# Seven quarter products in place of eight for the feed-forward weight product of the last three groups

## The chip, the core and the metric

The kernel runs on one core of a Trainium2 chip. The metric is the device time of one execution, in microseconds (us). All arithmetic is in 32-bit floats. The five engines have queues of their own: TensorE (PE in the profile) multiplies matrices into PSUM, VectorE (DVE), ScalarE (ACT) and GpSimd (POOL) work element by element, and SyncE (SP) issues DMA transfers.

## The reference, cut to what matters

Two layers work on 2 x 1024 tokens of width 256. Each layer has a cross-attention and a feed-forward step. The step that matters here is the first layer's feed-forward, in which the tokens are cut into 8 groups of 256, each with weights of its own, and nothing nonlinear stands between the two products:

```python
xg = x.reshape(8, 256, 256)
h1 = einsum('gmh,goh->gmo', xg, W1) + b1[:, None, :]     # W1: 8 x 1024 x 256
h2 = einsum('gmo,gho->gmh', h1, W2) + b2[:, None, :]     # W2: 8 x 256 x 1024
x = x + h2                                               # xg is layernorm(x)
```

So the two weights of a group can be multiplied once, into a matrix M of 256 x 256 (summed over the 1024 inner features), and the group's tokens then need one product with M. Before it stands the first layer's attention, behind it the second layer's attention over 64 context rows and a slot feed-forward with soft dispatch and combination.

## The kernel before, in words

**Tiling.** Tokens lie in four quads `xq[q]` of 128 partitions x 4 tiles x 256 features; a quad holds two feed-forward groups. A group's weights come as one tile `wg` of 128 partitions x 8 chunks (`oc`) x 513 elements: 256 elements of the first weight (`w1g`, the bias b1 folded into its first column), 256 of the second (`w2g`), and one column that is subtracted from the first weight by `prepare` (line 869, eight ScalarE instructions for each group from the second on). Three buffers take the eight groups in turn, so the load of a group waits until the product three groups earlier is done.

**The weight product.** `product(g)` makes M in PSUM: for each of 8 chunks and each of 2 halves of the rows, one TensorE matmul with a 128x128 block of `w1g` as the stationary operand and 128x256 of `w2g` streaming (line 882), 16 in all. A 32-bit matmul shows as two rows in the trace, so a product counts 32. Then one copy moves M to the SBUF tile `mt` (line 890), GpSimd adds b2 to one row (line 891), and `prepare` works on the next group.

**What stands around it.** The program is written as one sequence of calls; a scheduler moves the instructions of each engine within it by their dependences, except where an order is kept by hand. The part that matters runs as follows:

```python
        product(4); load_layer1(); norm_ff(1); attend(3)
        product(5); feed_forward(1)
        product(6); norm_ff(2); feed_forward(2)
        slot_norms(); norm_queries(0); product(7)
        norm_ff(3); norm_queries(1); norm_queries(2)
```

`norm_ff(q)` makes a layernorm of a quad on VectorE (`hn_f`, with the reciprocal root `rstd` on GpSimd, lines 124 and 125) and turns it by TensorE (`pt_f`). `feed_forward(q)` multiplies it with the two M of the quad (line 910) and adds the result to the tokens on VectorE (line 917). `norm_queries(q)` is the next layernorm (`hn_a`): VectorE normalizes (line 818) and turns 32x32 squares (`tr_a`, line 137); SyncE moves those out to DRAM (`d_a`, line 170) and back (`hTa`, line 172).

**The attention loop behind it.** For each quad it runs over two halves c. `queries` makes `pq` (line 1240) and the scores `psg` (line 1308), ScalarE takes a tanh, TensorE makes `poT` (line 1340), VectorE writes that to `oT` (line 1347), and `output` multiplies `oT` of both halves with the output weight into `pf` (line 1254), which VectorE adds to the tokens (line 1262). In the first quad's second half stands `norm_queries(3)`, kept in program order, ahead of the `oT` of that half on VectorE.

**The same scheme elsewhere.** The last feed-forward already makes its products by seven quarter products. `sum_rights` (lines 607 to 615) makes sums of quarters there with four VectorE instructions of 128x512, and the products have 128 columns (line 586).

Of the kernel before, what the change touches and what calls it, by code (L numbers as in the profile page):

```python
# [9 lines left out]
FP = mybir.dt.float32  # L10
AF = mybir.ActivationFunctionType
ALU = mybir.AluOpType
# [3 lines left out]
P = 128  # L16
B = 2
S = 1024
D = 256
DC = D // P  # L20
# [14 lines left out]
OC = FF // P  # L35
# [17 lines left out]
def tile_kernel(  # L53
# [19 lines left out]
    nc = tc.nc  # L73
# [9 lines left out]
    def bank(name, side=0):  # L83
        return ps[side].tile([P, 512], FP, tag="bank", name=name)
# [511 lines left out]
    def tt(dst, x, y, op):  # L596
        nc.vector.tensor_tensor(dst, x, y, op)  # L597
# [201 lines left out]
    with (  # L799
# [34 lines left out]
        ffc = wide.enter_context(tc.tile_pool(name="ffc", bufs=1))  # L834
        weights = {}

        def load_group(g, parts=(OC,)):


            wg = wff.tile([P, OC, 2 * D + 1], FP, tag="wg", name=f"wg_{g}")  # L840
            i = 0
            for n in parts:
                nc.sync.dma_start(out=wg[:, i : i + n], in_=wff_in[g, :, i : i + n])
                i += n
            weights[g] = wg[:, :, 0:D], wg[:, :, D : 2 * D], wg[:, :, 2 * D :]
# [10 lines left out]
        def prepare(g):  # L856
            if g not in weights:
                load_group(g)
            w1g, _, first = weights[g]
            less = ffc.tile([P, OC], FP, name=f"less_{g}")  # L860
            for part, scalar in enumerate((g > 0, g > 0)):
                ocs = range(part * OC // 2, (part + 1) * OC // 2)
                some = slice(ocs.start, ocs.stop)
                if scalar:
                    nc.scalar.activation(less[:, some], first[:, some, 0], AF.Copy, scale=-1.0)
                for oc in ocs:
                    w = w1g[:, oc, 1:]
                    if scalar:
                        last_prepared[g] = nc.scalar.activation(  # L869
                        w, w, AF.Identity, bias=less[:, oc : oc + 1]  # L870
                    )
                    else:
                        nc.vector.tensor_scalar(w, w, first[:, oc, :], None, ALU.subtract)  # L873

        def product(g):
            if g == 0:
                prepare(0)
            w1g, w2g, _ = weights[g]
            pm = bank(f"pmt_{g}", 1)
            for oc in range(OC):  # L880
                for hc in range(DC):
                    nc.tensor.matmul(  # L882
                        pm[:, ts(hc, D)],
                        lhsT=w1g[:, oc, ts(hc, P)],
                        rhs=w2g[:, oc, :],
                        start=(oc == 0 and hc == 0),
                        stop=(oc == OC - 1 and hc == DC - 1),
                    )
            mt = ffc.tile([P, DC, D], FP, name=f"mt_{g}")
            nc.any.tensor_copy(mt, pm.rearrange("p (c n) -> p c n", c=DC))  # L890
            nc.gpsimd.tensor_tensor(mt[0:1, 0, :], mt[0:1, 0, :], b2r[:, g, :], ALU.add)
            mts.append(mt)
            if g + 1 < NG:
                prepare(g + 1)


        hTfs = {}

        def norm_ff(q, side=0):
            out = nc.any.tensor_copy if q < QB else nc.scalar.copy  # L900
            hTfs[q] = layernorm(xq[q], f"f0_{q}", side, out)

        def feed_forward(q, side=0):
            for i in range(QN // GN):
                g = q * (QN // GN) + i
                xg = xq[q][:, ts(i, 2), :]
                po = bank(f"po_{g}", side)
                for t in range(2):
                    for dc in range(DC):
                        nc.tensor.matmul(  # L910
                            po[:, ts(t, D)],
                            lhsT=hTfs[q][:, dc, ds(i * GN + t * P, P)],
                            rhs=mts[g][:, dc, :],
                            start=(dc == 0),
                            stop=(dc == DC - 1),
                        )
                nc.vector.tensor_tensor(
                    xg, xg, po.rearrange("p (t d) -> p t d", t=2), ALU.add
                )
# [7 lines left out]
        with tc.tile_pool(name="p0", bufs=1) as p0, tc.tile_pool(name="a0", bufs=2) as a0:  # L927
# [25 lines left out]
            load_quad(3)  # L953

            product(0)


# [22 lines left out]
            for c in range(C0):  # L980
                for dc in range(DC):
                    nc.tensor.matmul(
                        pk[:, ts(c, P)],
                        lhsT=wk0s[:, dc, ts(c, P)],
                        rhs=hcT[:, dc].rearrange("p b j -> p (b j)"),
                        start=(dc == 0),
                        stop=(dc == DC - 1),
# [5 lines left out]
            for c in range(C0):  # L993
                for dc in range(DC):
                    nc.tensor.matmul(
                        pv[:, ts(c, P)],
                        lhsT=wv0s[:, dc, ts(c, P)],
                        rhs=hcT[:, dc].rearrange("p b j -> p (b j)"),
                        start=(dc == 0),
                        stop=(dc == DC - 1),  # L1000
# [9 lines left out]
            for dc in range(DC):  # L1010
                pws = [bank(f"pwk_{dc}_{e}") for e in range(2)]
                for c in range(C0):
                    for e in range(2):
# [3 lines left out]
                            lhsT=wq0s[r, c, ts(dc, P)],  # L1017
                            rhs=kT[r, c, :],
                            start=True,
                            stop=True,  # L1020
# [8 lines left out]
            for g in range(NBW // 2):  # L1029
                pw = bank(f"pvw_{g}")  # L1030
                for i in range(2):
                    for c in range(C0):
                        nc.tensor.matmul(
                            pw[ds(32 * c, 32), ts(i, D)],
                            lhsT=vblk[:, c, 2 * g + i].rearrange("p e j -> p (e j)"),
                            rhs=wo0s[:, c, :],
                            start=True,
                            stop=True,
# [52 lines left out]
            def turn_weights(q):  # L1091
                atf = ats[q].rearrange("p g j -> p (g j)")
                pat = bank(f"pat_{q}")
                for t in range(QT):
                    nc.tensor.transpose(pat[:, ts(t, P)], atf[:, ts(t, P)], ident)
                atT = a0.tile([P, QN], FP, tag="atT", name=f"atT_{q}")
                nc.scalar.copy(atT, pat)
                atTs[q] = atT

            def attend(q):  # L1100
                if q not in atTs:
                    turn_weights(q)
                atT = atTs[q]
                for i in range(2):
                    po = bank(f"po0_{q}_{i}")
                    for k in range(2):
                        t = 2 * i + k
                        nc.tensor.matmul(  # L1108
                            po[:, ts(k, D)],
                            lhsT=atT[:, ts(t, P)],  # L1110
                            rhs=vw[:, (q * QT + t) // 2, :],
                            start=True,
                            stop=True,
                        )
                    xi = xq[q][:, ts(i, 2), :]
                    nc.vector.tensor_tensor(
                        xi, xi, po.rearrange("p (t d) -> p t d", t=2), ALU.add
                    )

            weigh(0)  # L1120
            product(1)
            turn_weights(0)
            weigh(1)
            attend(0)
            product(2)
            turn_weights(1)
            weigh(2)
# [7 lines left out]
            load_layer1()  # L1135
            norm_ff(1)
            attend(3)
        product(5)
        feed_forward(1)
        product(6)  # L1140
        norm_ff(2)
        feed_forward(2)

        with (
            tc.tile_pool(name="a1c", bufs=1, side="right") as a1c,
# [35 lines left out]
            for c in range(C1):  # L1181
                for dc in range(DC):
                    nc.tensor.matmul(
                        pk[:, ts(c, P)],
                        lhsT=wk1s[:, dc, ts(c, P)],
                        rhs=ctxd[:, dc],
                        start=(dc == 0),
                        stop=(dc == DC - 1),
# [13 lines left out]
            for dc in range(DC):  # L1202
                nc.tensor.matmul(
                    pv[:, 0:D],
                    lhsT=ctxd[:, dc].rearrange("p b s -> p (b s)"),
                    rhs=wv1s[:, dc, :],
                    start=(dc == 0),
                    stop=(dc == DC - 1),
# [5 lines left out]
            for b in range(B):  # L1214
                for e in range(2):
                    to = vblk1[e * NK : (e + 1) * NK, b, :, e, :]
# [63 lines left out]
            for c in range(C1):  # L1280
                nc.tensor.matmul(
                    pvs[:, ts(c, B)],
                    lhsT=vals[:, ts(c, NPR)].rearrange("p r e d -> p (r e d)"),
                    rhs=in_batch,
                    start=True,
                    stop=True,
# [7 lines left out]
            for q in range(NQ):  # L1294
                b = q * QN // S
                oTs[q] = a1.tile([P, C1, QN], FP, tag="oT", name=f"oT_{q}")
                for c in range(C1):
# [8 lines left out]
                    for j in range(NPR):  # L1306
# [3 lines left out]
                            lhsT=kblk[r, c, b].rearrange("p e s -> p (e s)"),  # L1310
                            rhs=qTs[q][r, c, :],
                            start=True,
                            stop=True,
# [25 lines left out]
                    for j in range(NPR):  # L1339
                        nc.tensor.matmul(  # L1340
                            po[ds(32 * j, 32), :],
                            lhsT=vblk1[:, b, NPR * c + j].rearrange("p e d -> p (e d)"),
                            rhs=sg[:, j, :],
                            start=True,
                            stop=True,
# [153 lines left out]
```

## Time and profile before

| | |
|---|---|
| median of 3 runs | 423.4 us (423.31 to 423.4) |
| the profiled execution's own time | 423.25 us |
| its span, first to last instruction | 421.5 us |
| TensorE busy | 415.9 us, 99% of the span |
| VectorE busy | 315.6 us, 75% |
| ScalarE busy | 131.1 us, 31% |
| GpSimd busy | 74.1 us, 18% |
| granted TensorE clock | 1.000 |
| `pmt` matmuls of all 8 products (line 882) | 256 rows, 58.3 us |
| products 5, 6 and 7 on TensorE | start at 69.80, 82.03 and 95.37 us, 6.91 us each |

The span is the time that the profile sees; 1.75 us of the execution lie around it. Busy times are sums over the whole span; the durations of TensorE rows are modelled and overlap, so the distance from start to start says more than a row's own duration. In a row of the timeline stand the start, the time from first start to last end of its instructions, the engine, the source line, the operation with the tile that it writes and the tiles that it reads, their shapes, the count, and in brackets the idle time ahead of it with what ended it.

### The profile page before, as it was taken

The page shows a single profiled execution, that of the slowest core. Times are in us where ns is not written, and L with a number is a line of the kernel's source. Part 1 is how long each engine was busy: PE and PEld are TensorE (multiplying, and loading weights), DVE is VectorE, ACT ScalarE, POOL GpSimd, SP SyncE. Part 2 cuts the span into 40 slices and gives each one's busy share as a digit, 9 for nine tenths or more (in the row PEclk, how much of TensorE's full clock was granted, in tenths as well). Part 3 has the DMA queues.
Part 4 walks back from the last instruction along what each step waited for, and adds up shares of the span by engine and source line. Part 5 has one row for each costly group of instructions (what it writes and reads, how often), then busy time and mean ns, then how long its engine had stood idle before and what let it go on. Part 6 is the DMA issues. An engine that isn't in the chain of part 4 may idle for free.

```text
span 421.5 us, 6298 instructions
## 1 busy us (share of the span) xinstructions
PE 415.9 (99%) x2270; PEld 310.3 (74%) x2270; DVE 315.6 (75%) x711; ACT 131.1 (31%) x266; POOL 74.1 (18%) x86
## 2 busy tenths in 40 slices
PE   8999999999999999999999999999999999999996
PEld 7889988888444454444488644899998864499996
DVE  2677777745578669978769889977985589776956
ACT  1145938513544522344641654300000004420000
POOL 2113233211101220104948900000000000000000
PEclk9999999999999999999999999999999999999999
DMA  6999983413633332120052764450022576520003
GB/s 256 416 415 425 402 340 134 168 47 112 149 102 105 46 47 31 29 43 2 0 213 101 129 97 74 65 89 2 0 84 49 121 120 98 89 44 2 2 2 100
DMA packets 99425, 50.03 MB, mean 119 GB/s; under 512 B 87873, under 2 KB 94401, under 8 KB 97857
## 3 DMA queue, kind: packets, MB, share of 16 engines
q1 hardware_dynamic: 99394, 49.63, 42.2%
q8 instruction: 18, 0.29, 0.3%
q14 instruction: 13, 0.11, 0.1%
HBM read 32.74 MB, written 6.30 MB: 93 GB/s over the span
## 4 chain that ended last, share of the span: by engine, by line
PE 86%; DVE 7%; SPq 2%; DMA 2%; issue 1%; POOL 1%; ACT 0%; DVEq 0%
PE psl L409 13%; PE pmt L882 13%; PE pc L586 12%; PE pp L586 12%; PE pmh L511 10%; PE pl L256 7%; PE pq L1240 3%; PE po L910 3%; SPq L158 2%; PE psc L1058 2%; PE pf L1254 2%; PE po L1108 2%; PE psg L1308 2%; PE poT L1340 1%; DMA wg<-in_wff_dram 1%
## 5 line engine op out<-in xcount | busy, mean ns | idle before, releaser
L882 PE MATMUL pmt<-wg 128*128 128x256 f32 x256 | 58.3, 384 | 0.3 <-DVE wg L873 0.3
L409 PE MATMUL psl<-xh,lg 128*128 128x258 f32 x256 | 56.8, 381 | 0.0
L256 PE MATMUL pl<-seT,xhT 128*128 128x512 f32 x128 | 56.1, 594 | 0.2 <-DVE rmax L275 0.2
L882 PEld LDWEIGHTS pmt<-wg 128*128 128x128 f32 x256 | 48.8, 193 | 7.5 <-DVE wg L873 0.7
L409 PEld LDWEIGHTS psl<-xh,lg 128*128 128x128 f32 x256 | 48.2, 190 | 7.4 <-issue 0.5
L256 PEld LDWEIGHTS pl<-seT,xhT 128*128 128x128 f32 x128 | 24.1, 190 | 29.2 <-issue 25.7
L395 POOL TENSOR_TENSOR lg<-lg,mb 128x1024 f32<-128x1024 f32 x13 | 33.2, 2594 | 26.9 <-ACT mb L203 25.3
L279 ACT ACTIVATE ec<-lg,nm 128x1024 f32<-128x1024 f32 x16 | 18.4, 1149 | 39.7 <-DVE nm L264 37.7
L586 PEld LDWEIGHTS pp<-ms,mh 128*128 128x128 f32 x256 | 29.4, 192 | 1.6 <-issue 1.0
L586 PE MATMUL pp<-ms,mh 128*128 128x128 f32 x256 | 30.2, 276 | 0.3
L521 ACT ACTIVATE mh<-mh 128x512 f32<-128x512 f32 x32 | 19.2, 627 | 21.1 <-DVE mh L557 19.6
L511 PE MATMUL pmh<-slT,ms 128*128 128x512 f32 x48 | 24.2, 592 | 0.0
L869 ACT ACTIVATE wg<-wg,less 128x255 f32<-128x255 f32 x56 | 23.4, 495 | 0.1
L1317 ACT ACTIVATE sg<-psg 128x512 f32<-128x512 f32 x32 | 16.5, 603 | 18.2 <-PE psg L1308 18.2
L586 PE MATMUL pp<-m_sums,mh 128*128 128x128 f32 x192 | 22.1, 275 | 0.0
L586 PE MATMUL pc<-pr,ec 128*128 128x128 f32 x192 | 22.1, 275 | 0.0
L586 PEld LDWEIGHTS pc<-pr,ec 128*128 128x128 f32 x192 | 21.8, 192 | 0.0
L586 PEld LDWEIGHTS pp<-m_sums,mh 128*128 128x128 f32 x192 | 21.8, 192 | 0.0
L398 ACT ACTIVATE lg<-lg 128x1024 f32<-128x1024 f32 x16 | 16.1, 1045 | 18.3 <-POOL lg L395 18.3
L545 ACT COPY mh<-pmh 128x512 f32<-128x512 f32 x8 | 4.6, 569 | 50.2 <-PE pmh L511 50.2
L308 DVE STREAM_TRANSPOSE tr<-ec 128x512 f32<-128x512 f32 x32 | 19.7, 674 | 0.0
L597 DVE TENSOR_TENSOR mh<-mh,mh 128x1024 f32<-128x1024 f32 x16 | 18.5, 1218 | 0.5 <-PE pp L586 0.5
(193 smaller groups left out, 669.8 us busy)
## 6 DMA issues: line engine op xcount, KB each, us to landing
wg<-in_wff_dram SPq DMA_DIRECT2D x5, 2052.0 KB, 10.1
ec<-tr SPq DMA_DIRECT2D x128, 64.0 KB, 2.3
wg<-in_wff_dram SPq DMA_DIRECT2D x4, 1026.0 KB, 12.9
xT<-in_xT_dram SPq DMA_DIRECT2D x4, 512.0 KB, 13.9
x<-in_x_dram SPq DMA_DIRECT2D x4, 512.0 KB, 16.1
d_a<-tr_a SPq DMA_DIRECT2D x4, 512.0 KB, 2.6
hTa<-d_a SPq DMA_DIRECT2D x16, 128.0 KB, 3.1
xhT<-tr_m SPq DMA_DIRECT2D x64, 32.0 KB, 2.0
```

The source lines that it names most:

```text
L256: nc.tensor.matmul(pl, lhsT=xhTs[q][:, dc, ts(t, P)], rhs=in_order(seT[:, n], dc), start=(dc == 0), stop=(dc == DC - 1),)
L279: nc.scalar.activation(ecs[q][:, :, t, :], lg.rearrange("p (h n) -> p h n", h=2), AF.Exp, bias=nm[:, 1:2], scale=-1.0, accum_out=zcs[b][:, ...
L308: ins = nc.vector.transpose(tr[:, :, :, t, :].rearrange("p r c n -> p c r n"), half[:, t, :].rearrange("p (c r n) -> p c r n", c=EC // 2, ...
L395: engine.tensor_tensor(lgs[b][s], lgs[b][s], mbs[b], ALU.add)
L409: nc.tensor.matmul(pz[:, 0:XW], lhsT=lgs[b][s][:, ts(c, P)], rhs=xhs[b * QB + s // QT][:, s % QT, :], start=(s == 0), stop=(s == ST - 1),)
L511: nc.tensor.matmul(to, lhsT=lefts[i][:, ts(j, P)], rhs=in_order(slTs[b][0], i) if i < 2 else rights[b][i], start=True, stop=True,)
L521: nc.scalar.activation(h, h, AF.Gelu)
L586: nc.tensor.matmul(to, lhsT=left(k, m), rhs=right[:, k, :], start=(k == 0), stop=(k == QT - 1),)
L597: nc.vector.tensor_tensor(dst, x, y, op)
L869: last_prepared[g] = nc.scalar.activation(w, w, AF.Identity, bias=less[:, oc : oc + 1])
L882: nc.tensor.matmul(pm[:, ts(hc, D)], lhsT=w1g[:, oc, ts(hc, P)], rhs=w2g[:, oc, :], start=(oc == 0 and hc == 0), stop=(oc == OC - 1 and hc ...
L1317: nc.scalar.activation(sg[:, j, :], psgs[j], AF.Tanh, scale=0.5 * DH1**-0.5)
```

## The change

For groups 5, 6 and 7, M is no longer summed from 16 matmuls of 256 columns. Both weights are cut into quarters: by halves of the 8 chunks and by halves of their 256 columns. `sum_quarters(g)` makes the sums and differences of quarters on VectorE, eight instructions of 128x512, four of the second weight and four of the first. Two of the eight are written over a quarter of the weight itself, six into a new tile `qs`. `product_of_quarters(g)` makes seven products of quarters, each of four matmuls of 128 columns, 28 in all, in two PSUM banks. ScalarE copies the first product to SBUF, and seven VectorE additions of 128x128, each with one operand in PSUM, put the four quarters of `mt` together. `sum_quarters(g + 1)` is called at the end of `product(g)`, behind `prepare(g + 1)`. The `qs` of groups 5 and 7 share a buffer of the pool `ffc`; that of group 6 lies in a new pool `qp`, which is opened ahead of `product(5)` and closed behind `feed_forward(2)`.

```diff
+        FEWER = (5, 6, 7)
+        HO = OC // 2
+        quarter_sums, sums_in = {}, [ffc]
+        def quarters(w):
+            return [[w[:, ts(k, HO), ts(i, P)] for i in range(2)] for k in range(2)]
+        def sum_quarters(g):
+            w1g, w2g, _ = weights[g]
+            qs = sums_in[-1 if g == 6 else 0].tile([P, 6, HO, P], FP, tag="qs", name=f"qs_{g}")
+            s1, s2, s4, t1, t2, t4 = (qs[:, i] for i in range(6))
+            (b11, b12), (b21, b22) = quarters(w2g)
+            tt = nc.vector.tensor_tensor
+            tt(t1, b12, b11, ALU.subtract)
+            tt(t2, b22, t1, ALU.subtract)
+            tt(b12, b22, b12, ALU.subtract)
+            tt(t4, b21, t2, ALU.subtract)
+            (a11, a21), (a12, a22) = quarters(w1g)
+            tt(s1, a21, a22, ALU.add)
+            tt(s2, s1, a11, ALU.subtract)
+            tt(a21, a11, a21, ALU.subtract)
+            tt(s4, a12, s2, ALU.subtract)
+            quarter_sums[g] = [
+                (a11, b11), (a12, b21), (s2, t2), (a21, b12), (s1, t1), (s4, b22), (a22, t4)
+            ]
+        def product_of_quarters(g):
+            pms = [bank(f"pmt_{g}_{i}", 1) for i in range(2)]
+            p1, p2, p6, p7, p5, p3, p4 = (
+                pms[i // 4][:, ts(i % 4, P)] for i in range(7)
+            )
+            for to, (left, right) in zip((p1, p2, p6, p7, p5, p3, p4), quarter_sums[g]):
+                for k in range(HO):
+                    nc.tensor.matmul(to, lhsT=left[:, k, :], rhs=right[:, k, :],
+                                     start=(k == 0), stop=(k == HO - 1))
+            mt = ffc.tile([P, DC, D], FP, name=f"mt_{g}")
+            u = ffc.tile([P, 3, P], FP, tag="u", name=f"u_{g}")
+            (c11, c12), (c21, c22) = [[mt[:, c, ts(i, P)] for i in range(2)] for c in range(2)]
+            u1, u2, u3 = (u[:, i] for i in range(3))
+            tt = nc.vector.tensor_tensor
+            nc.scalar.copy(u1, p1)
+            tt(u2, p6, u1, ALU.add)
+            tt(c11, p2, u1, ALU.add)
+            tt(u3, p7, u2, ALU.add)
+            tt(c22, p5, u3, ALU.add)
+            tt(u2, p5, u2, ALU.add)
+            tt(c12, p3, u2, ALU.add)
+            tt(c21, p4, u3, ALU.add)
+            return mt
...
         def product(g):
...
+            if g in FEWER:
+                mt = product_of_quarters(g)
+            else:
                 pm = bank(f"pmt_{g}", 1)
...
             if g + 1 < NG:
                 prepare(g + 1)
+                if g + 1 in FEWER:
+                    sum_quarters(g + 1)
...
+        qp = ExitStack()
+        sums_in.append(qp.enter_context(tc.tile_pool(name="qp", bufs=1)))
         product(5)
         feed_forward(1)
         product(6)
         norm_ff(2)
         feed_forward(2)
+        qp.close()
```

More of the change, by code (lines that the diff above doesn't have):

```diff
@@ new lines, in product_of_quarters @@
+        def product_of_quarters(g):
[5 more added lines that the diff above has]
+                for k in range(HO):
+                    nc.tensor.matmul(
+                        to,
+                        lhsT=left[:, k, :],
+                        rhs=right[:, k, :],
+                        start=(k == 0),
+                        stop=(k == HO - 1),
+                    )
+            mt = ffc.tile([P, DC, D], FP, name=f"mt_{g}")
[12 more added lines that the diff above has]
+            return mt
@@ L878, in product @@
             w1g, w2g, _ = weights[g]
[L879 to L890, printed above, removed]
+            if g in FEWER:
+                mt = product_of_quarters(g)
+            else:
+                pm = bank(f"pmt_{g}", 1)
+                for oc in range(OC):
+                    for hc in range(DC):
+                        nc.tensor.matmul(
+                            pm[:, ts(hc, D)],
+                            lhsT=w1g[:, oc, ts(hc, P)],
+                            rhs=w2g[:, oc, :],
+                            start=(oc == 0 and hc == 0),
+                            stop=(oc == OC - 1 and hc == DC - 1),
+                        )
+                mt = ffc.tile([P, DC, D], FP, name=f"mt_{g}")
+                nc.any.tensor_copy(mt, pm.rearrange("p (c n) -> p c n", c=DC))
             nc.gpsimd.tensor_tensor(mt[0:1, 0, :], mt[0:1, 0, :], b2r[:, g, :], ALU.add)
```

## The prediction

> **What bounds the kernel now.** I read the page's shares first, then the chain of waits for 76 to 125 us, then VectorE's timeline for the same time, since what the change adds lies there.
>
> ```profile
> PE 415.9 (99%) x2270; PEld 310.3 (74%) x2270; DVE 315.6 (75%) x711; ACT 131.1 (31%) x266; POOL 74.1 (18%) x86
> ```
>
> TensorE has hardly a gap in the span: what it saves is time won, as long as nothing else makes it wait. The chain runs through it without a break in the changed stage (start, length, what):
>
> ```profile
> 82.03 6.91 PE pmt L882 x32
> ...
> 95.37 6.91 PE pmt L882 x32
> ...
> 113.82 3.63 PE pq L1240 x8
> 117.45 1.00 PE poT L1340 x8
> 118.45 1.07 PE psg L1308 x8
> 119.52 3.65 PE pf L1254 x16
> ...
> 290.11 25.01 PE pc L586 x224
> ```
>
> VectorE has room there, but it is in pieces that wait for TensorE (in brackets), and in short ones that wait for GpSimd's root:
>
> ```profile
> 60.10 0.69 DVE L1070 TENSOR_TENSOR e<-psc,mx 128x512 f32<-128x512 f32 x1
> ...
> 89.92 1.56 DVE L818 TENSOR_SCALAR hn_a<-x,mv_a,rstd_a 128x256 f32<-128x256 f32 x4 [6.17 <-PE pt_f L133]
> ...
> 103.53 0.16 DVE L1288 TENSOR_SCALAR vsum<-pvs 128x4 f32<-128x4 f32 x1 [3.58 <-PE pvs L1281]
> ...
> 110.07 0.69 DVE L917 TENSOR_TENSOR x<-x,po 128x512 f32<-128x512 f32 x1 [3.46 <-PE po L910]
> ...
> 115.74 1.38 DVE L818 TENSOR_SCALAR hn_a<-x,mv_a,rstd_a 128x256 f32<-128x256 f32 x4 [1.48 <-POOL rstd_a L125]
> ...
> 118.59 0.75 DVE L1347 TENSOR_SCALAR oT<-poT,vsum 128x512 f32<-128x512 f32 x1
> ```
>
> The last row is the second half of `oT`. It ends at 119.34, and the second matmul of `pf`, which needs it, starts at 119.52 + 0.43 = 119.95: VectorE is ready with 0.6 us to spare.
>
> **TensorE's side.** A product is 16 matmuls in 6.91 us, 0.432 each. A 128-column matmul with a new stationary block each time is in the row of `pc`: 224 rows are 112 matmuls in 25.01 us, 0.2233 each. 28 of them take 6.25 us. Each product is shorter by 0.66 us, three by **1.98 us**. That is 0.66 less than the eighth of each product (0.86): two half-width matmuls cost more than one wide. No order but the products' changes on TensorE. `pf` would start at 117.54, and its second matmul at 117.97, if nothing makes it wait.
>
> **VectorE's side.** Three groups add 24 sums of 128x512 and 21 additions of 128x128. The price is from start to start, since neighbours overlap:
>
> ```profile
> 247.32 0.68 DVE L561 TENSOR_TENSOR mh<-mh,pmh 128x512 f32<-128x512 f32 x1
> 247.92 0.68 DVE L563 TENSOR_TENSOR mh<-mh,pmh 128x512 f32<-128x512 f32 x1
> ...
> 266.19 0.68 DVE L610 TENSOR_TENSOR m_sums<-ms 128x512 f32<-128x512 f32 x1
> 266.91 1.42 DVE L597 TENSOR_TENSOR m_sums<-ms,m_sums 128x512 f32<-128x512 f32 x2
> 268.24 0.68 DVE L597 TENSOR_TENSOR ms<-ms 128x512 f32<-128x512 f32 x1
> 268.84 2.48 DVE L308 STREAM_TRANSPOSE tr<-ec 128x512 f32<-128x512 f32 x4
> ```
>
> An independent one starts 0.60 after the one before. One that reads its neighbour's result starts 0.72 after it; the last four lines are the same four-instruction pattern of sums elsewhere, 2.65 us or 0.66 each. In the changed order other work stands between most dependent pairs, so I take 0.60, with 0.66 as the dear end: 24 x 0.60 = **14.4 us** (15.8). There is no 128x128 `TENSOR_TENSOR` in the trace. From 512 to 256 columns the distance falls from 0.60 to 0.33 (`ggb`, 68.76 to 69.09), which goes on to 0.20 at 128; the three-operand form with 128 columns (line 750) takes 15 in 4.29 us, 0.28 each. I take 0.20, the same operation, and keep 0.28: 21 x 0.20 = **4.2 us** (5.9).
>
> Now the queue from line 1070's start at 60.10 to the second `oT`. Before, its instructions at these distances sum to 34.5 us: 20 `BN_STATS` at 0.32, 20 aggregates at 0.09, 24 of lines 818 at 0.315, 20 turned squares at 0.345, 4 `se` at 0.40, 15 of 512 columns at 0.61, and 1.0 of small ones. The rest of 58.5 us is standing: 16.0 us in six waits ahead of TensorE work or `sn`, 5.9 in four waits of 1.47 for `rstd`, 2.1 in gaps below 0.8. After, one copy of `hT_f` (0.6) goes to ScalarE: 34.5 - 0.6 + 14.4 + 4.2 = **52.5 us**. The added work does not just fill the gaps: it makes the queue late, so every wait for TensorE goes. The waits for `rstd` don't, because in the changed order little stands between each `mv` and its `hn`: five of them, 1.45 for `hn_f` of quad 2, 1.05 for `hn_f` of quad 3 (three small instructions between), 1.15 for `hn_a` 1, 1.4 for `hn_a` 2 (GpSimd first adds b2 to `mt` 7, 0.72), 1.45 for `hn_a` 3: 6.5 us. Short gaps: 1.0, fewer than before as there are fewer waits. The second `oT` starts at 60.10 + 52.5 + 6.5 + 1.0 = **120.1**, ends at 120.85, and the second `pf` matmul goes at 120.9 in place of 119.95. So **+0.95 us**: TensorE gains 1.98 by 117.97 and then waits 2.9 us. What is behind `oT` in VectorE's queue is the addition of `pf` itself, which comes as much later; the order behind it is that of before, so the 0.95 goes through to the end.
>
> [...] The rows at 247.32 and 247.92 start 0.60 apart with 0.68 each, so I go by the rows.
>
> **What else moves.** Within products, TensorE needs the sums from the third quarter product on. Counting the queue on: group 5's eighth sum ends near 69 (needed at 74), group 6's `s2` near 81.8 and the last near 82.8 (needed at 83.1), group 7's near 90.5 (needed at 95.5). Group 6 has 1.3 us of cover; a wait there costs nothing more until it passes the 2.9 us that TensorE loses anyhow. ScalarE: three copies of 128x512 (0.59) become three of 128x128; `sq` of `slot_norms` now waits for the last `po0` at 72.5, since its memory is used until then, so `wg` 6 is prepared near 79.3 in place of 75.4, 2 us before product 6. GpSimd: the clearing of `vblk` (0.52) and three small ones move behind the same `po0`; nothing needs them before 95. SyncE: `tr_a` 0 ends near 91.5 in place of 74.9, so `d_a` 0 and `hTa` 0 go out then, with `vblk`'s two moves now between; at 3.2 us and 3.1 us to landing and 0.43 an issue, `hTa` 0 lands near 101, and `pq` 0 wants it at 101.5. `hTa` 1 lands near 111.3 for 111.8. Both may cost some tenths, inside the same 2.9 us. PSUM: a product holds two of four banks, and `po` 6 waits for the last addition into `mt` 7, near 105 for 106.
>
> **The rivals.**
> - *Dear additions.* At 0.66 and 0.28 the queue is 1.4 + 1.7 us later: +2.6 to +4.1 us, 426.0 to 427.5. For it: PSUM operands, many dependent pairs. Against: rows of line 917 with PSUM (0.68) cost as much as those without. Chance 0.23; beyond +4.1 another 0.03, if quarters at a pitch of 513 elements ran like the slow one of `sl_sums` (line 498, 1.41 against 0.69 for its twin).
> - *VectorE in time (the other side).* If the second `oT` ends by 118.0, 2.9 us earlier than counted, TensorE keeps all 1.98: 421.3 us. It is faster by over 0.2% (0.85 us, about what a measurement can tell from no change) once `oT` ends by 119.1, 1.8 earlier. The place is the queue between 95 and 120, where 6.5 us are waits for GpSimd: two of them covered by sums would do. For it: only 5% of the queue's 60 us are in question. Against: the order is fixed, and between these `mv` and `hn` it has no sums. Chance of +0.0 down to -0.85 0.10, of less 0.07.
> - *No saving at all.* If a 128-column matmul were paced by its own duration (275 ns against 379), products would be 1.6 us longer. The chain's distances exclude it.
>
> **How the numbers follow.** The sum is made against the profiled execution's own 423.25 us, which is 0.15 below the median: 424.2 to 424.4, so 424.4. Cases: +0.0 to +1.9 around the count 0.57 (0.27 of it within 0.85), dear 0.23 + 0.03, in time 0.17. Faster 0.07, the same 0.10 + 0.27 = 0.37, slower 0.30 + 0.26 = 0.56. The range goes from -0.4 (some of the in-time case) to the dear end at +3.7 us: 423.0 to 427.1.
>
> **What would show it.** Right: three products of 6.25 us, starting near 69.8, 81.4 and 94.0; VectorE waiting only for `rstd` from 66 to 120; sums 0.60 and additions 0.20 apart; a wait of 2 to 4 us of `pf` for `oT`, line 1347 becoming line 1412, and none of over 1 us before it. Wrong: a product longer than 6.5 us with waits for `qs`, waits for `hTa`, or `pf` starting before 119.

## The result, and the profile after

The changed kernel took 428.74 us (median of 426.52, 429.94, 429.46 and 428.02), the kernel before 423.36 in the same session: ratio 1.0124, 95% interval 1.0078 to 1.0169. It is slower, and the median lies above the forecast range. Run again later, the same kernel gave 426.25 us in six executions (424.61 to 427.87) against 423.25, ratio 1.0069 (1.0052 to 1.0087); that median lies inside the range. Executions of the kernel before lie within 0.4 us of its median; those of the changed one spread over 5.3 us. That spread is the first sign of what the forecast lacked.

The profiled execution of after took 426.52 us with a span of 424.6, against 423.25 and 421.5. From the page, the shares and the row of the granted clock:

```profile
PE 415.6 (98%) x2342; PEld 311.8 (73%) x2342; DVE 333.2 (78%) x755; ACT 130.9 (31%) x267; POOL 74.9 (18%) x86
...
PEclk9999999999989999999999999999999999999999
```

The clock row has an 8 in its twelfth slice of forty, 117 to 127 us; the page of before has only nines. TensorE's timeline of after (start, length, what, and the idle time ahead of it):

```profile
81.57 1.95 PE L910 MATMUL pmt<-wg 128*128 128x128 f32 x16
...
94.21 1.95 PE L910 MATMUL pmt<-wg 128*128 128x128 f32 x16
...
117.79 0.70 PE L1319 MATMUL pf<-w1s,oT 128*128 128x256 f32 x2
121.60 4.97 PE L1319 MATMUL pf<-w1s,oT 128*128 128x256 f32 x14 [3.11 <-DVE oT L1412]
```

In the same view of before, all 16 rows of `pf` stand in one piece:

```profile
119.45 3.72 PE L1254 MATMUL pf<-w1s,oT 128*128 128x256 f32 x16
```

Up to `pf` TensorE is 1.7 us ahead of before (117.79 against 119.45). Then it stands for 3.11 us, waiting for the second `oT`. And then something that no step of the forecast has: the other 14 rows of `pf` take 4.97 us. At full clock 14 such rows take 3.29 (the run with three sums in experiment 2). The stretches around that place, from the view by windows (columns: stretch and its length, then busy time and instructions of TensorE, its weight loads, VectorE, ScalarE, GpSimd; the granted clock; the DMA share and rate):

```profile
120.00:121.50 1.50, 0.00 (x0) 0.00 (x0) 1.50 (x4) 0.00 (x0) 0.00 (x0) 1.00 0.01 1
121.50:123.00 1.50, 1.40 (x5) 1.17 (x6) 0.05 (x1) 0.00 (x0) 0.00 (x0) 0.72 0.84 339
123.00:125.00 2.00, 2.00 (x6) 1.65 (x5) 0.91 (x2) 0.00 (x0) 0.00 (x0) 0.50 0.12 33
125.00:127.00 2.00, 2.00 (x14) 1.10 (x13) 1.14 (x5) 0.00 (x0) 0.00 (x0) 0.86 0.71 227
```

The clock falls to 0.50 behind the wait. The stretches at its edges show a mean (0.72 over 1.5 us, 0.86 over 2.0); with 0.50 in the slow part, it was halved from 122.16 to 125.56, 3.40 us. The account of this execution against before: the second matmul of `pf` starts at 121.60 instead of one matmul after 119.45, at 119.88, so +1.7, of which 0.3 was there at 57.9 us already, ahead of the first sum; the 14 rows at a slow clock add 4.97 - 3.29 = 1.7. That is +3.4 at the end of `pf`; the span is 3.1 longer.

VectorE's queue, in its timeline of after:

```profile
77.67 0.28 DVE L923 TENSOR_TENSOR u<-pmt,u 128x128 f32<-128x128 f32 x1
77.87 0.27 DVE L924 TENSOR_TENSOR mt<-pmt,u 128x128 f32<-128x128 f32 x1
...
78.27 0.67 DVE L891 TENSOR_TENSOR wg<-wg 128x512 f32<-128x512 f32 x1
78.86 0.68 DVE L892 TENSOR_TENSOR qs<-wg,qs 128x512 f32<-128x512 f32 x1
...
81.19 1.23 DVE L895 TENSOR_TENSOR qs<-qs,wg 128x512 f32<-128x512 f32 x1
82.34 0.69 DVE L896 TENSOR_TENSOR wg<-wg 128x512 f32<-128x512 f32 x1
...
118.20 1.38 DVE L818 TENSOR_SCALAR hn_a<-x,mv_a,rstd_a 128x256 f32<-128x256 f32 x4 [1.48 <-POOL rstd_a L125]
...
120.84 0.71 DVE L1412 TENSOR_SCALAR oT<-poT,vsum 128x512 f32<-128x512 f32 x1
```

Sums start 0.60 apart and additions, each with an operand in PSUM, 0.20; a sum right behind the one whose result it reads starts 0.72 after it (61.00 and 61.72 us). The queue is full but for the waits for `rstd`, and the second `oT` starts 0.7 us behind the count of 120.1 (0.6 in the second profile, at 120.71).

**Theories.** *Clock theory*: a TensorE wait of about 3 us costs its length and also a halved clock for one or more stretches like the 3.40 us of this profile, each worth up to 1.7 us (half of it); how many differs from one execution to the next. By an estimate from the mean clocks of the four executions (0.996, 0.988, 0.992 and 0.992, over spans of 425 to 428 us) they had one, three, two and two such stretches at half the clock. *Rival*: the loss lies in the sums and additions or in the changed order, and the clock only accompanies it.

### The profile page after: what moved, and what is told of

It is laid out like the page before. It is cut to its first block, busy times and chain, and to the rows that moved or that the text cites. A ratio compares the mean times of both kernels' runs of the same rounds, so it can differ in the third digit from the quotient of the medians.

```text
span 424.6 us, 6494 instructions
## 1 busy us (share of the span) xinstructions
PE 415.6 (98%) x2342; PEld 311.8 (73%) x2342; DVE 333.2 (78%) x755; ACT 130.9 (31%) x267; POOL 74.9 (18%) x86
## 4 chain that ended last, share of the span: by engine, by line
PE 68%; DVE 19%; SPq 4%; DMA 3%; POOL 2%; issue 2%; ACT 0%; DVEq 0%; POOLq 0%
PE pc L586 12%; PE pp L586 11%; PE psl L409 10%; PE pmh L511 9%; PE pl L256 7%; PE pmt L942 6%; SPq L158 2%; PE pf L1319 2%; SPq L325 2%; PE psc L1120 2%; PE pq L1305 2%; DMA wg<-in_wff_dram 1%; DVE tr_a L137 1%; DVE lg L264 1%; DVE hn_a L818 1%
## 5 line engine op out<-in xcount | busy, mean ns | idle before, releaser
L942 PE MATMUL pmt<-wg 128*128 128x256 f32 x160 | 36.6, 385 | 0.7 <-DVE wg L873 0.7
L942 PEld LDWEIGHTS pmt<-wg 128*128 128x128 f32 x160 | 30.4, 193 | 5.6 <-DVE wg L873 1.4
L1319 PE MATMUL pf<-w1s,oT 128*128 128x256 f32 x64 | 17.4, 422 | 3.2 <-DVE oT L1412 3.1
L1319 PEld LDWEIGHTS pf<-w1s,oT 128*128 128x128 f32 x64 | 12.8, 208 | 10.1 <-DVE oT L1412 4.4
```

What stands on the lines that cost most here:

```text
L942: nc.tensor.matmul(pm[:, ts(hc, D)], lhsT=w1g[:, oc, ts(hc, P)], rhs=w2g[:, oc, :], start=(oc == 0 and hc == 0), stop=(oc == OC - 1 and hc ...
L1319: nc.tensor.matmul(pf[:, ts(k, D)], lhsT=oTs[q][:, c, ts(2 * i + k, P)], rhs=wo1s[:, c, :], start=(c == 0), stop=(c == C1 - 1),)
```

## The experiments

**1. The wait filled.** The changed kernel with work for TensorE where it stood:

```diff
                     pf = bank(f"pf_{q}_{i}", 1)
+                    if q == 0 and i == 0:
+                        for _ in range(14):
+                            nc.tensor.matmul(pf[:, 0:P], lhsT=wo1s[:, 0, 0:P],
+                                             rhs=wo1s[:, 1, 0:P], start=True, stop=True)
```

> The changed kernel, with 14 added matmuls of 128x128 float32 (14 x 0.223 = 3.1 us) on TensorE in the place of its wait at the first `pf`; they write into the `pf` bank that the real matmuls then write anew. Nothing is made earlier: the second `oT` still ends near 121.5 us. Clock theory: the clock stays 1.00 behind it, the 14 real `pf` matmuls take 3.2 us instead of 4.97, and the time is 424.5 to 425.1 us with runs within 0.5 us. Rival (the clock has nothing to do with the wait): 427 to 430 us and the same scatter as the changed kernel.

Measured: 425.26 us (425.07 to 425.60, five executions), ratio to before 1.0047 (1.0035 to 1.0059). Mean clock 1.000 in all five. TensorE's timeline of it:

```profile
117.52 3.39 PE L1319 MATMUL pf<-w1s 128*128 128x128 f32 x28
120.74 3.87 PE L1328 MATMUL pf<-w1s,oT 128*128 128x256 f32 x16
```

The second `oT` is about as late as without the filling (it starts at 120.55, there at 120.84), yet more work on TensorE makes the kernel 1 to 3.5 us faster than its two medians, and the spread is gone (the kernel before took 423.25 to 423.36 in the three sessions). All five executions kept the clock; unfilled, three of ten did (experiment 4), and these took 424.61 to 426.09, so the filling takes away the slow clock and not the wait's length. The rival said 427 to 430; it falls. The time is 0.2 above the upper end expected.

**2. Sums alone, without any product of seven.** In the kernel before, with n = 3, 5, 6 or 9:

```diff
-                    nc.vector.tensor_scalar(
-                        oTs[q][:, c, :], po, 0.5, vsum[:, c, b : b + 1], ALU.mult, ALU.add
+                    if c == 1 and q == 0:
+                        for _ in range(n):
+                            tc.keep_in_program_order(nc.vector.tensor_tensor(
+                                oTs[0][:, 1, :].rearrange("p (t d) -> p t d", t=2),
+                                xq[0][:, 0:2, :], xq[0][:, 2:4, :], ALU.add))
+                    tc.keep_in_program_order(nc.vector.tensor_scalar(
+                        oTs[q][:, c, :], po, 0.5, vsum[:, c, b : b + 1], ALU.mult, ALU.add
+                    ))
```

> The kernel before, with 3 sums of 128x512 on VectorE (0.60 us apart, 1.8 us) right ahead of the second `oT`, whose place they write and which writes over them; TensorE's work is unchanged. The second `oT` has 0.6 us of slack, so TensorE waits 1.2 us at `pf`. Both theories: 1.2 us more than before, 424.3 to 424.7 us. Clock theory further: a wait this short leaves the granted clock at 1.00 and the runs within 0.5 us; if it halved too, 426 us or more with scatter.

> The kernel before, with 6 such sums (3.6 us) ahead of the second `oT`: a wait of 3.0 us at `pf`, as long as the changed kernel's, without any product of seven. Clock theory: granted clock of 0.5 for some 3.4 us behind the wait, 1.7 us and more above the wait: 428 to 431 us, with runs over 1 us apart. Rival (the wait costs only its length): 426.3 us, runs within 0.5 us, clock 1.00.

> The kernel before with 5 sums ahead of the second `oT`. The six took 4.28 us (0.72 us apart) and made TensorE wait 3.42 us, so five make it wait 2.7 us. By the length alone (no clock): 423.25 + 2.7 = 425.9 to 426.2 us. Clock theory: somewhere between the 1.25 us that left the clock at 1.00 and the 3.1 us that did not, it starts to fall; if 2.7 us is enough, executions at 0.996 lie 1.7 us higher, at 427.6 or so, beside others at 426.

> The same with 9 sums: 9 x 0.72 = 6.4 us, a wait of 5.6 us at `pf`. By the length alone 428.9 to 429.3 us, all runs within 0.5 us. Clock theory: every execution loses at least one stretch of half the clock, so no mean clock above 0.997 and 430.5 to 434 us, with scatter in steps of some 1.7 us.

The row of `pf` behind its wait, in TensorE's timelines with 3, 5 and 9 sums (with 6 it is 4.78 us behind 3.42):

```profile
121.31 3.29 PE L1254 MATMUL pf<-w1s,oT 128*128 128x256 f32 x14 [1.25 <-DVE oT L1355]
```

```profile
122.84 4.94 PE L1254 MATMUL pf<-w1s,oT 128*128 128x256 f32 x14 [2.70 <-DVE oT L1355]
```

```profile
125.78 4.90 PE L1254 MATMUL pf<-w1s,oT 128*128 128x256 f32 x14 [5.60 <-DVE oT L1355]
```

| sums | wait, us | time, us (lowest to highest) | above before | mean clock of the executions |
|---|---|---|---|---|
| 3 | 1.25 | 424.33 (424.19 to 424.45) | 1.1 | 0.999 to 1.000, all 8 |
| 5 | 2.70 | 427.36 (425.50 to 428.66) | 4.1 | one 1.000, four 0.995 to 0.996, one 0.991 |
| 6 | 3.42 | 428.02 (426.97 to 429.04) | 4.8 | one 1.000, two 0.996, one 0.992 |
| 9 | 5.60 | 431.03 (430.24 to 431.89) | 7.8 | 0.992, all 4 |

A wait of 1.25 us costs 1.1 us and nothing else, so keeping the order of every `oT` by hand, which the edit also does, costs nothing of its own. With 2.70, 3.42 and 5.60 us the same 14 rows take 4.94, 4.78 and 4.90 us instead of 3.29, and the median is 1.3 to 2.2 us above the wait's length. With 2.70 and 3.42 us a single execution each kept the clock, and it cost its wait within 0.5 us (425.50 and 426.97). So the seven-product change is not needed for the effect; a late `oT` is enough. Six sums took 4.28 us and not the 3.6 expected of them, hence a wait of 3.42 for 3.0; their median lies at the low end of the clock theory's figure.

The mean clock alone does not give the price. In the profile with nine sums, by windows:

```profile
121.50:123.00 1.50, 0.00 (x0) 0.00 (x0) 1.43 (x3) 0.13 (x1) 0.00 (x0) 0.75 0.39 96
...
129.00:131.00 2.00, 2.00 (x12) 1.30 (x14) 1.69 (x6) 0.00 (x0) 0.00 (x0) 0.98 0.00 0
```

With 0.50 in all windows between, the clock was halved from 122.2 to 129.1, 6.8 us, twice the 3.40 of the first profile. For the first 3.5 us of it TensorE stood anyway, so the 14 rows are no slower than with five sums. The lowest time, 430.24 us, is 0.3 below what the clock theory had expected.

**3. Six sums, and the wait filled** with the 14 matmuls of experiment 1.

> The same with 6 sums, and with 14 added matmuls of 128x128 (3.1 us) on TensorE in the place of the wait, overwritten by the real ones. The second `oT` is as late as without them. Clock theory: clock 1.00, the time rises by the lateness alone: 426.2 to 426.8 us, runs within 0.5 us, and 2 us or more under the same kernel unfilled. Rival: the same time as unfilled.

Measured: 427.14 us (426.91 to 427.64), mean clock 0.999 to 1.000 in all four. The level is 0.3 above the range expected, for the longer six sums; it is what the unfilled kernel took in its one execution at full clock (426.97). The median falls by only 0.9 where 2 or more was expected, since of the four unfilled executions one lost nothing and only one had a clock as low as 0.992. The direction speaks for the clock theory, the size is smaller than I wrote.

**4. The changed kernel again.**

> The changed kernel again, unaltered, for more executions and a second profile. Clock theory: the executions differ by their mean granted clock, and each 0.004 of it (1.7 us of a span of 425 us) costs about 1.7 us above a floor of some 425 us, which is what the filled kernel takes at 1.000; the profile shows one or more stretches of about 3.4 us at half the clock behind the wait at `pf`. Rival: differences in time without a difference in clock, or a low clock that stands elsewhere than behind the wait.

All ten executions of it, by mean granted clock: 1.000: 424.61, 425.61, 426.09; 0.996: 426.41, 426.49, 426.52; 0.992: 427.87, 428.02, 429.46; 0.988: 429.94 us. The groups do not overlap; their means are 425.4, 426.5, 428.5 and 429.9, 1.0 to 2.0 us apart for each 0.004. The new profile is of the one at 0.992, by windows:

```profile
120.00:121.50 1.50, 0.01 (x1) 0.01 (x1) 1.43 (x4) 0.00 (x0) 0.00 (x0) 0.77 0.01 1
...
125.00:127.00 2.00, 2.00 (x6) 1.58 (x5) 1.11 (x5) 0.00 (x0) 0.00 (x0) 0.50 0.77 228
127.00:129.00 2.00, 2.00 (x14) 0.55 (x17) 1.14 (x3) 0.00 (x0) 0.00 (x0) 0.84 0.02 5
```

A wait of 3.01 us, about the same as in the first profile, and here the clock is halved from 120.8, while TensorE still stands, to 127.6: 6.8 us, twice 3.4. The 14 rows of `pf` take 6.30 us. So the length of the wait alone does not decide between one stretch and two. What does, no run shows. At clock 1.000 the kernel still spreads over 1.5 us, which the theory does not explain.

**5. The change for two groups.** `FEWER = (6, 7)`.

> The change for groups 6 and 7 alone (two products of seven, 16 sums and 14 additions). TensorE gains 2 x 0.66 = 1.3 us; VectorE has about 8 x 0.60 + 7 x 0.20 = 6.2 us less added to its queue, which is more than the 3.1 us by which it came late. Clock theory: no wait at `pf`, clock 1.00, 421.9 to 422.3 us. Rival (the cost sits in the sums and additions themselves, in proportion): two thirds of the changed kernel's loss, 425 to 427 us.

Measured: 422.06 us (421.74 to 422.23), ratio 0.9968 (0.9957 to 0.9980), mean clock 0.999 to 1.000. `oT` starts at 117.17, and TensorE runs through `pf` without a gap:

```profile
118.03 3.72 PE L1319 MATMUL pf<-w1s,oT 128*128 128x256 f32 x16
```

It gains 1.24 us of the 1.32 that two shorter products are worth, and is faster than both kernels. Two thirds of the change do not cost two thirds of the loss: that rival falls too.

**6. The norm moved out of the way**, in the changed kernel and in the kernel before.

```diff
                 for c in range(C1):
-                    if c == 1 and q == 0:
-                        norm_queries(3, True)
...
-                    nc.vector.tensor_scalar(
+                    ot = nc.vector.tensor_scalar(
                         oTs[q][:, c, :], po, 0.5, vsum[:, c, b : b + 1], ALU.mult, ALU.add
                     )
+                    if c == 1 and q == 0:
+                        with tc.issue_after(ot.ins):
+                            norm_queries(3, True)
```

> The changed kernel, with the norm of the last 512 queries (its statistics, 4 `hn` and 4 transposes) put behind the second `oT` in VectorE's queue; no other engine's order changes. Clock theory (the 3.1 us TensorE wait costs its length and then halves the granted clock for some 3.4 us, again another such stretch in longer executions): the wait at the first `pf` disappears, the clock stays 1.00 there, and TensorE's gain of 1.7 to 2.0 us is left: 421.4 to 421.9 us, all runs within 0.3 us. Rival (the loss is not in this wait: the sums or additions cost elsewhere, or another order behind it): still 424 us or more, with the scatter of the changed kernel.

> The kernel before with the same move of the norm of the last 512 queries behind the second `oT`. Both theories: there is no wait at `pf` to take away, so 423.2 to 423.6 us; a gain of over 0.5 us here would say that the move helps by itself and that the first experiment shows less than it seems to.

Measured: 422.83 us (421.94 to 423.98, ratio 0.9990, 0.9981 to 1.0000) in the changed kernel; 424.54 (424.27 to 424.65) in the kernel before. Both expectations missed by about 1 us, for one reason: the norm then stands ahead of the fourth `oT`, and the next `pf` waits. In TensorE's timeline of the changed kernel with the move:

```profile
117.38 3.72 PE L1319 MATMUL pf<-w1s,oT 128*128 128x256 f32 x16
...
130.44 3.29 PE L1319 MATMUL pf<-w1s,oT 128*128 128x256 f32 x14 [0.95 <-DVE oT L1410]
```

No wait at the first `pf`, 0.95 us at the second (1.0 in the kernel before with the same move). With the same queue of norms and no long wait in either, seven products instead of eight save 424.54 - 422.83 = 1.71 us by the medians. The two profiles agree: in their chains of waits `poT` ahead of the first `pf` starts at 115.38 against 117.41, and the 14 rows behind the second wait at 130.44 against 132.49, 2.0 us earlier both times. The 1.71 is rough, though: executions at 422.2 and at 423.9 stand side by side in the changed kernel with clocks of 0.997 to 1.000, and what parts them is open.

**7. `turn_slot_rows` moved as well**, behind the fourth `oT`.

```diff
-                    if c == 1 and q == 1:
-                        turn_slot_rows(1)
...
+                    if c == 1 and q == 1:
+                        with tc.issue_after(ot.ins):
+                            turn_slot_rows(1)
```

> The changed kernel with the norm of the last 512 queries behind the second `oT` (as in the first experiment, which turned the wait at the first `pf` into one of 0.9 us at the second), and now the second half of `turn_slot_rows` (4 `se`, 4 transposes, 2.9 us) behind the fourth `oT` too, which that wait was for. Theory that VectorE's queue alone holds the gain back: no wait over 0.3 us at any `pf`, clock 1.00, 421.2 to 421.9 us. Rival (what is pushed back is late for something else, such as the logits that need `seT`): 422.5 us or more with a wait there.

Measured: 424.96 us (423.69 to 425.40, ratio 1.0032, 1.0020 to 1.0043). No wait at any `pf`, but in the view of waits:

```profile
PE pl L256 <- DMA xhT<-tr_m: 1.6, 1, 1.6
```

The first logits (`pl`) wait for `xhT`, whose source `tr_m` VectorE now starts at 134.15 us instead of 132.88 in experiment 6. The rival was right: pushed further, the lateness comes out at a transfer.

**8. Eight of the sums on GpSimd**, on `w1g` of groups 5 and 7.

```diff
             (a11, a21), (a12, a22) = quarters(w1g)
+            if g != 6:
+                tt = nc.gpsimd.tensor_tensor
```

> The changed kernel, with the four sums on `w1g` of groups 5 and 7 on GpSimd instead of VectorE (8 of the 24 sums; about 1.3 us each there, half of its 2.59 us for 128x1024). VectorE is rid of 8 x 0.60 = 4.8 us ahead of the second `oT`, more than the 3.1 us that it was late; TensorE's order is unchanged. Clock theory: no wait at `pf`, clock 1.00, TensorE's 2 us kept: 421.2 to 421.9 us, runs within 0.5 us. Rival (GpSimd's sums slow VectorE's or come late for a product, so a wait stays or a new one takes its place): 422.5 us or more.

Measured: 431.25 us (430.20 to 432.74), ratio 1.0192 (1.0172 to 1.0212). TensorE's waits:

```profile
PE pq L1307 <- DVE u L927: 5.3, 1, 5.3
PE pmt L912 <- DVE qs L897: 1.8, 1, 1.8
```

Two waits ahead of `pf` take the place of the one there, and the mean clock is 0.990 to 0.995. The GpSimd sums took 1.2 to 1.7 us each, and two of VectorE's sums beside them took 1.67 and 1.76 us. In VectorE's timeline of it:

```profile
89.83 1.67 DVE L891 TENSOR_TENSOR wg<-wg 128x512 f32<-128x512 f32 x1
```

The same line took 0.67 us in the changed kernel. Here a sum on GpSimd ran beside it from 89.29 to 90.95 us, and VectorE's ended 0.55 after that. The rival was right here: the time is far above the 422.5 us at which it began.

## Why the forecast was wrong

**TensorE's saving** was right: products 6 and 7 take 6.25 us each; the three start at 69.93, 81.57 and 94.21 (foretold near 69.8, 81.4 and 94.0), and `pf` at 117.79 for 117.54. The execution was 0.3 late ahead of all of them. The medians say 1.71 us in experiment 6 against 1.98, and 1.24 for two groups against 1.32.

**VectorE's prices and waits** were right: 0.60 and 0.20, and five waits for `rstd` of 1.48, 1.10, 1.16, 1.25 and 1.48 us, 6.47 against 6.5. The second `oT` was foretold at 120.1 and came at 120.84, 0.3 of it from the start of the execution. For the other 0.44 there are two instructions that grew beside GpSimd: the sum at 81.19 (1.15 us to the next instead of 0.60, while GpSimd adds b2 to `mt` 5 from 81.15) and one `se` at 105.57 (0.83 long, where the count had 0.40, beside the same for `mt` 7). The count had no term for that. Together they grew by 0.98, more than the 0.44, so other terms of the count were too large by about 0.5; which ones stays open. Sums of 0.68 us started 0.60 apart, additions of 0.28 us 0.20 apart. The rival of dear additions and the one of VectorE in time are both excluded by these rows.

**The covers** held: no wait for `qs`, `hTa` or PSUM ahead of `pf`, as foretold for the signs of right.

**The failed step** is the last of the sum: "TensorE gains 1.98 by 117.97 and then waits 2.9 us", from which "the 0.95 goes through to the end". The wait was there, 3.11 and 3.01 us in the two profiles. But it was priced at its length. Its price is its length plus the slow clock behind it: the 14 rows of `pf` took 4.97 and 6.30 us in the two profiles for 3.29 at full clock, so 1.7 us more for one stretch and 3.0 for two, and in three executions of ten there was no slow clock at all. For the first profile the account closes: the late queue adds 0.7 and the clock 1.7, 2.4 in all, and the execution took 426.52 where the sum, on its own base of 423.25, had 424.2. Without the slow clock the times come near the sum's 424.4: 424.6 to 426.1 in those three executions, 425.26 in the filled kernel. The term was also missing from the rivals, so the range ended at 427.1, below four of the ten executions and below the first median (and below the 427.5 of its own rival of dear additions). All the signs of being right came, and the time was still missed, since none of them looked at the clock. That the kernel would be slower, to which the prediction gave 0.56, came true by the wait that it foretold and by the clock that it did not. The page of before could not show it: it has no wait of over 1.0 us on TensorE and no slice under 9 in the clock row.

In the traces the clock falls to half (0.50) and stays there for 3.40 us in the first profile, 3.41 with five sums, 3.4 with six and 6.8 in two profiles. Whether it falls changes from one execution to the next: the mean clock of the changed kernel was 1.000 in three of ten, 0.988 to 0.996 in seven. A wait of 1.25 us left the mean clock at 0.999 to 1.000 in all eight executions; with one of 2.70 us it was 0.991 to 0.996 in five of six. In the second profile of the changed kernel the clock fell 2.3 us after TensorE stopped. How long TensorE has to stand for it, no run shows.

## What to carry to other kernels

Price a wait of the engine that sets the end by its length plus what the clock does behind it: here 1.25 us of waiting cost 1.1, 2.7 us cost 4.1. Before moving work to a second engine, find the first place where the first engine waits for it, and stop where that wait begins: two groups gained 1.24 us, the third turned it into a loss. When executions of one kernel scatter and those of its neighbour don't, read the granted clock of each before looking for a cause in the order of work.

## What was not expected of the hardware

- More work made the kernel faster: 14 matmuls with no use, put into the wait, took the median from 426.25 or 428.74 to 425.26 us and the spread from 5.3 to 0.5.
- The slow stretches were 3.40 us long (first profile), 3.41 (five sums) and 3.4 (six sums), or 6.8, twice that (second profile, nine sums). In the first profile the clock fell 0.6 us after TensorE had resumed (122.16, work from 121.60), in the second while it stood (120.8), and there it stayed at 0.50 until 127.6 although TensorE worked from 121.5 on. In these five profiles TensorE had stood for 2.1 to 3.1 us when the clock fell. What sets the length of a stretch and the moment of its start, no run shows.
- Beside GpSimd's sums, two of VectorE's sums in experiment 8 took 1.67 us (at 89.83) and 1.76 (at 91.42), with all operands in SBUF; the same two took 0.67 and 0.68 in the changed kernel. Each ended 0.55 us after the GpSimd sum that had started before it (90.95 and 92.63 us), about the time of a sum by itself (0.60 from start to start). One at 89.25, with a GpSimd sum from 89.29 on, took 0.65. Why the two grew, no run shows.
